# The mask of a causal attention added by TensorE: two full-array products per step against eight in 32x32 tiles

## The chip, the core and the metric

The kernel runs on one NeuronCore of a Trainium2 chip. The metric is the device time of one execution in microseconds (us). Engines are named as in the profile: PE is TensorE (its matmuls), PEld its weight loads, DVE is VectorE, ACT is ScalarE, POOL is GpSimd and SP is SyncE, whose queue issues most of the DMAs.

## What is computed

The reference is a two-layer block on x of shape 16 x 128 x 256 (16 batches of 128 tokens): a first attention with fp8-rounded projections, a gated feed-forward, a second attention, and a feed-forward over 8 experts. The change touches the second attention alone:

```
scores = einsum("bnghd,bmgd->bnghm", q, k) / sqrt(8)      # 32 heads of width 8, in 8 groups of 4
scores = where(attention_mask == 0, -inf, scores)          # per key of the batch
scores = where(tril(ones(128, 128)), scores, -inf)         # causal
attn = softmax(scores); out = einsum("bnghm,bmgd->bnghd", attn, v) @ w_o.T + b_o
```

## The kernel before

The second attention runs as a software pipeline over 64 steps n. Step n belongs to batch b = n // 4 and covers 8 of the 32 heads, as two groups of four. Four batches form a group g, for which `load`, `norm`, `turn` and `queries` (the front, spread over 16 steps by `front_step`) bring keys, values and queries into SBUF. The pipeline loop (L1291) calls for each n, in this order: `scores(n)`, `top(n)`, `probs(n - 1)`, `exp(n)`, `values(n - 2)`, `divide(n - 5)`, every fourth step `keys` of the next batch, then a piece of the next front, pieces of the routing for the experts (`route`), and every fourth step `output`. During the first steps, `down` finishes the feed-forward before.

The steps that matter here, by line:

- `load(g)` makes on DVE `pad` (L1062), which is 0 or -1e30 per key, and `comb` (L1063), the elementwise minimum of `pad` and the causal mask: 128 queries on the partitions, 4 batches x 128 keys in bf16, once per group.
- `scores(n)` fills a PSUM tile `ps_sc` of two banks, one for each group i of four heads, with 512 float32 per partition. First the mask goes in: for each i one bf16 matmul of the identity (`identb`, 128x128) with `comb` broadcast over four heads (L1141). Then the scores are added: for each i one float32 matmul with 32 contraction rows (L1148), which lie on the partitions 32 * (2p + i), where p = n % 2. A float32 matmul shows as two MATMUL records.
- `top(n)` takes on DVE the negated maximum per head (L1155). `exp(n)` is eight activations on ACT (L1164), one per head, which read `ps_sc` directly. `probs(n)` transposes the eight results on PE (L1175), and DVE (L1179) or, for a quarter of them, ACT (L1177) copies them out as `eT`.
- `values(n)`, for odd n, is four float32 matmuls with 32 output columns each (L1203): their results go to four different quarters of the PSUM partitions. ACT copies them out (L1209), and they go through DRAM and back to `divide` (L1236 on DVE, L1237 on POOL). `output` is L1243 on PE, `queries` L1103, `turn` L1092; the transposes of `route` are L159.
- `keys(b)` makes `kb` for a batch on POOL (L1118), the keys of a group multiplied with a head mask.

`ps_sc` has two buffers, `ps_tr` two, `ps_pv` one, `comb` two. The framework writes the order on each engine out ahead of time, from the priority in which the program issues instructions and from planned durations; the score matmuls get a raised priority (`tc.high_priority(offset=100)`). So each engine has a fixed order, and PE takes its matmuls in that order.

Of the kernel before, what the change touches and what calls it, by code (L numbers as in the profile page):

```python
# [9 lines left out]
F32 = mybir.dt.float32  # L10
F32R = mybir.dt.float32r
BF16 = mybir.dt.bfloat16
# [3 lines left out]
ALU = mybir.AluOpType  # L16
AX = mybir.AxisListType

P = 128
# [5 lines left out]
NEG = -1e30  # L25
# [10 lines left out]
def flamingo_kernel(  # L36
# [27 lines left out]
    nc = tc.nc  # L64
# [212 lines left out]
    with (  # L277
# [88 lines left out]
        class Unit:  # L366
# [15 lines left out]
            def load(self):  # L382
                b = self.b
                if self.cross:
                    cx = ap.tile([P, KD, P], F32, tag="ctx", name="ctx")
                    nc.sync.dma_start(out=cx, in_=kpn(ctxT)[:, :, b * P : (b + 1) * P])
                    xx = ap.tile([P, KD * P], F32R, tag="xx", name="xx")
                    nc.sync.dma_start(out=xx.bitcast(F32), in_=xqx[b])
                    self.kv_lhs = [cx[:, k, :] for k in range(KD)]
                    self.q_lhs = [xx[:, k * P : (k + 1) * P] for k in range(KD)]  # L390
# [160 lines left out]
            def scores(self, c):  # L551
                qT = self.qT.pop(c)
                pscore = ps_sc([P, 4, P])
                for j in range(4):
                    nc.tensor.matmul(  # L555
                        pscore[:, j, :], qT[:, j, :], self.kT[:, 2 * c + j // 2, :],
                        start=True, stop=True,
                    )
                self.sc[c] = pscore
# [244 lines left out]
    G = 4  # L804
    NT = G * P
# [75 lines left out]
    NQ = NH // NG  # L881
# [9 lines left out]
    for j in range(B):  # L891
# [9 lines left out]
        out=before, in_=ones, pattern=[[1, P]], compare_op=ALU.is_gt, fill=0.0,  # L901
        base=0, channel_multiplier=-1,
# [3 lines left out]
        rank, pattern=[[-1, NE]], base=NE, channel_multiplier=0,  # L906
# [4 lines left out]
        spare, pattern=[[P, B]], base=B * P, channel_multiplier=1,  # L911
# [10 lines left out]
    def route(b0, G):  # L922
# [73 lines left out]
    cq = f1.enter_context(tc.tile_pool(name="a1c", bufs=1, side="right", reuse_waits="tile"))  # L996
    gp = f1.enter_context(tc.tile_pool(name="a1f", bufs=2, side="right", reuse_waits="tile"))
# [7 lines left out]
    identb = cq.tile([P, P], BF16, name="identb")  # L1005
    nc.vector.tensor_copy(identb, ident)

    causal = cq.tile([P, P], F32, name="causal")
    nc.gpsimd.memset(causal, 0.0)
    nc.gpsimd.affine_select(  # L1010
        out=causal, in_=causal, pattern=[[-1, P]], compare_op=ALU.is_ge, fill=NEG,
        base=0, channel_multiplier=1,
    )

    hmask = cq.tile([P, NQ], F32, name="hmask")
    nc.vector.memset(hmask, 0.0)
    for q in range(P // 32):
# [3 lines left out]
            out=rows, in_=rows, pattern=[[-HD, NQ]], compare_op=ALU.is_ge, fill=0.0,  # L1021
            base=0, channel_multiplier=1,
        )
        nc.gpsimd.affine_select(
            out=rows, in_=rows, pattern=[[HD, NQ]], compare_op=ALU.is_ge, fill=0.0,
            base=HD - 1, channel_multiplier=-1,
# [16 lines left out]
    front = {}  # L1043

    def load(g):
        tok = slice(g * NT, (g + 1) * NT)
        kT = gp.tile([P, KD, NT], F32, tag="k", name="kT")
        for r in range(0, P, HD):
            q = r // 32
            nc.sync.dma_start(  # L1050
                out=kT[r : r + HD],
                in_=k1s.rearrange("(c q d) t -> q d c t", q=4, d=HD)[q][:, :, tok],
            )
        v = gp.tile([P, G, NG * HD], F32, tag="v", name="v")
        nc.sync.dma_start(out=v, in_=v1s[tok, :].rearrange("(b t) n -> t b n", t=P))
        mi = gp.tile([P, NT], I32, tag="mi", name="mi", bufs=1)
        nc.sync.dma_start(
            out=mi, in_=mask[g * NT : (g + 1) * NT].partition_broadcast(P)
        )
        comb = gp.tile([P, G, P], BF16, tag="comb", name="comb")  # L1060
        pad = gp.tile([P, NT], F32, tag="pad", name="pad", bufs=1)
        nc.vector.tensor_scalar(pad, mi, 0.0, NEG, ALU.is_equal, ALU.mult)  # L1062
        nc.vector.tensor_tensor(  # L1063
            comb, pad.rearrange("p (b t) -> p b t", b=G),
            causal[:, None, :].to_broadcast([P, G, P]), ALU.min,
        )
        front[g] = {"k": kT, "v": v, "comb": comb}

    def norm(g):
        rows = [x[b] for b in range(g * G, (g + 1) * G)]  # L1070
# [35 lines left out]
            )  # L1106
        nc.scalar.activation(f["q"][:, c, :], pm, AF.Copy, scale=SCALE1)

    kbs, vps, es, eTs, oTs, scs, mxs, ovs = {}, {}, {}, {}, {}, {}, {}, {}

    def keys(b):

        g, j = divmod(b, G)
        f = front[g]
        tok = slice(j * P, (j + 1) * P)
        kb = ap.tile([P, KD, NQ, P], F32, tag="kb", name="kb")
        for c in range(KD):
            nc.gpsimd.tensor_tensor(  # L1118
                kb[:, c], f["k"][:, c, None, tok].to_broadcast([P, NQ, P]),
                hmask[:, :, None].to_broadcast([P, NQ, P]), ALU.mult,  # L1120
            )
        v = f["v"][:, j, :].rearrange("p (g d) -> p g d", d=HD)
        if b < B - 1:
            nc.gpsimd.tensor_copy(vgs[b % 2][:, :, 0 : 2 * HD : 2], v)
        else:
            vp = vpad[:]
            nc.gpsimd.tensor_copy(
                bass.AP(vp.tensor, vp.offset, [vp.ap[0], [P, NG], [32 + HD, NQ], [1, HD]]),
                v[:, :, None, :].to_broadcast([P, NG, NQ, HD]),
            )  # L1130
        kbs[b], vps[b] = kb, vgs[b % 2]

    def scores(n):

        b, c, p = n // 4, n // 2 % 2, n % 2
        g, j = divmod(b, G)
        f = front[g]
        tok = slice(j * P, (j + 1) * P)
        s = psum.tile([P, 2, NQ, P], F32, tag="sc", name="ps_sc", bufs=2)
        for i in range(2):  # L1140
            nc.tensor.matmul(  # L1141
                s[:, i], identb, f["comb"][:, j, None, :].to_broadcast([P, NQ, P]),
                start=True, stop=False,
            )
        with tc.high_priority(offset=100):
            for i in range(2):
                rows = slice(32 * (2 * p + i), 32 * (2 * p + i) + 32)
                nc.tensor.matmul(  # L1148
                    s[:, i], f["q"][rows, c, tok], kbs[b][rows, c], start=False, stop=True
                )  # L1150
        scs[n] = s
# [105 lines left out]
    def front_step(g, i):  # L1257

        if i == 0:
            load(g)  # L1260
            norm(g)
        elif i == 3:
            turn(g)
        elif 5 <= i < 7:
            queries(g, i - 5)

    hds = {}
    for g in range(B // G):
# [3 lines left out]
        for b in range(g * G, (g + 1) * G):  # L1272
# [11 lines left out]
            name="psum1", bufs=1, space=bass.MemoryType.PSUM, reuse_waits="tile"  # L1284
# [6 lines left out]
    for n in range(-2, N1 + 2):  # L1291
        if 0 <= n < N1:
            scores(n)
            top(n)
# [14 lines left out]
        if m % 4 == 0 and 0 <= m < N1:  # L1309
            keys(m // 4)  # L1310
        g, i = divmod(n + 12, 16)
# [14 lines left out]
    for stages in routes:  # L1326
        for _ in stages:
# [6 lines left out]
            name="psum2", bufs=2, space=bass.MemoryType.PSUM, reuse_waits="tile"  # L1334
# [6 lines left out]
    for e in range(NE):  # L1341
# [6 lines left out]
            out=xe, in_=disp[e * CAP : (e + 1) * CAP, :].rearrange("(c p) d -> p c d", p=P)  # L1348
# [5 lines left out]
        for f in range(NFC):  # L1354
            ph = ps_mm([P, CAP])
            for k in range(KD):
                nc.tensor.matmul(
                    ph, w1t[:, k, f * P : (f + 1) * P], xT[:, k, :],
                    start=(k == 0), stop=(k == KD - 1),
# [3 lines left out]
        for c in range(NCC):  # L1363
            po = ps_sc([P, DM])
            for f in range(NFC):
                nc.tensor.matmul(
                    po, hT[:, f, c * P : (c + 1) * P], w2t[:, f, :],
                    start=(f == 0), stop=(f == NFC - 1),
# [6 lines left out]
                out=out_rows,  # L1375
# [3 lines left out]
                in_=oe[:, c, :],  # L1379
# [77 lines left out]
```

## Time and profile before

| | us |
|---|---|
| median of 3 runs | 1472.05 |
| the runs, from and to | 1471.78 to 1472.88 |
| the profiled execution's own time | 1470.57 |
| its span, first to last instruction | 1468.9 |
| TensorE clock granted, mean | 0.979 |
| second attention, L1141 from its first to its last start | 1044.4 to 1308.8 |

The profile is of one execution. "Busy" counts instructions of an engine; matmuls are pipelined and their ends are modelled, so a PE record is longer than the time until the next matmul may begin. What a matmul costs in a stream is therefore read from the starts: the start of the next instruction minus its own. The busy shares of the whole span are PE 93%, DVE 67%, ACT 57%, POOL 46%.

### The profile page before, as it was taken

The numbers are of one execution on the slowest core, as the hardware profiler recorded it, in microseconds if no ns is written. First come the engines' busy times: TensorE is split into PE (matmuls) and PEld (weight loads), VectorE is DVE, ScalarE is ACT, GpSimd is POOL, SyncE is SP. The second block draws the span as 40 slices with busy tenths as digits, with TensorE's granted clock in tenths as the row PEclk, the third lists the DMA queues.
The fourth block names the chain that finished last, engine by engine and source line by source line (L and its number), as shares of the span: only waits on it lengthen the run. The fifth ranks groups of instructions, "written<-read, shape, count | busy, mean of one in ns | idle before, by whom it ended". The sixth has DMA issues, their size and how long they took to land. (4 is left out here: it accounts for less than half of the span.)

```text
span 1468.9 us, 22241 instructions
## 1 busy us (share of the span) xinstructions
PE 1371.6 (93%) x7112; PEld 972.6 (66%) x7112; DVE 988.7 (67%) x2604; ACT 840.2 (57%) x2505; POOL 681.6 (46%) x641
## 2 busy tenths in 40 slices
PE   6799999999989899999999997999999999996998
PEld 5577787878766677777777765455544544455887
DVE  6788888887887677677776775453467877882110
ACT  5666666666656566666666663163467666751211
POOL 1576877777777456556556564121031422211111
PEclk9899999999999999999999999999999999996999
DMA  5201001000031100000000000700042222122562
GB/s 176 87 20 39 26 24 35 26 21 26 24 112 53 36 22 15 12 19 16 14 20 12 15 4 27 216 8 15 4 150 56 66 61 66 44 63 93 190 196 66
DMA packets 77844, 79.88 MB, mean 54 GB/s; under 512 B 15131, under 2 KB 63963, under 8 KB 77728
## 3 DMA queue, kind: packets, MB, share of 16 engines
q1 hardware_dynamic: 64224, 54.76, 13.0%
q10 hardware_dynamic: 11456, 17.63, 3.7%
q0 software_dynamic: 2048, 6.07, 1.1%
q8 instruction: 57, 0.93, 0.3%
q14 instruction: 59, 0.48, 0.1%
HBM read 56.88 MB, written 21.79 MB: 54 GB/s over the span
## 5 line engine op out<-in xcount | busy, mean ns | idle before, releaser
L525 POOL TENSOR_TENSOR raw<-raw,q_r 128x512 f32<-128x512 f32 x192 | 220.2, 1168 | 8.6 <-DVE q_r L340 7.6
L583 POOL TENSOR_TENSOR e<-e,sums 128x512 f32<-128x512 f32 x128 | 135.8, 1061 | 182.9 <-ACT raw L485 73.9
L571 ACT ACTIVATE e<-ps_sc,mx 128x128 f32<-128x128 f32 x512 | 181.1, 368 | 65.1 <-DVE mx L563 63.9
L494 DVE BATCH_NORM_STATS2 q_st<-raw 128x6 f32<-128x128 f32 x768 | 172.3, 278 | 59.2 <-ACT raw L485 58.9
L645 PE MATMUL ps_acc<-wp,cat 128*128 128x512 f32 x512 | 160.0, 435 | 18.4 <-POOL cat L260 17.5
L596 ACT COPY eT<-ps_tr 128x512 f32<-128x512 f32 x128 | 75.3, 588 | 171.4 <-PE ps_tr L594 171.4
L260 POOL TENSOR_TENSOR cat<-e_t,e_e 128x1024 fp32r<-128x1024 bf16 x64 | 136.6, 2135 | 53.2 <-DVE e_t L254 51.4
L1164 ACT ACTIVATE e<-ps_sc,mx 128x128 f32<-128x128 f32 x512 | 139.1, 391 | 27.2 <-DVE mx L1155 26.8
L555 PEld LDWEIGHTS ps_sc<-kT,qT 128*128 128x128 f32 x1024 | 132.2, 193 | 28.9 <-ACT qT L546 20.6
L555 PE MATMUL ps_sc<-kT,qT 128*128 128x128 f32 x1024 | 140.6, 280 | 6.6 <-ACT qT L546 6.5
L537 PE MATMUL ps_tr<-ident,raw 128*128 128x128 f32 x768 | 113.4, 277 | 24.1 <-ACT kT L546 15.3
L645 PEld LDWEIGHTS ps_acc<-wp,cat 128*128 128x128 f32 x512 | 93.7, 191 | 61.9 <-POOL cat L260 28.7
L604 PE MATMUL ps_pv<-eT,vt 128*128 128x256 f32 x512 | 133.1, 381 | 1.0 <-DVE cat_y L615 1.0
L537 PEld LDWEIGHTS ps_tr<-ident,raw 128*128 128x128 f32 x768 | 92.4, 142 | 56.3 <-issue 26.7
L485 ACT COPY raw<-ps_mm 128x512 f32<-128x512 f32 x192 | 113.7, 593 | 24.8 <-PE ps_mm L473 21.6
L604 PEld LDWEIGHTS ps_pv<-eT,vt 128*128 128x128 f32 x512 | 96.7, 191 | 31.2 <-issue 11.1
L615 DVE TENSOR_TENSOR cat_y<-ps_pv,r_sm 128x512 bf16<-128x512 f32 x128 | 87.1, 680 | 44.8 <-PE ps_pv L604 44.8
L546 ACT ACTIVATE qT<-ps_tr,hv 128x512 f32<-128x512 f32 x128 | 101.5, 793 | 20.4 <-PE ps_tr L537 16.7
L571 ACT ACTIVATION_READ_ACCUMULATOR e<-ps_sc,mx 128x1 f32 x512 | 105.3, 206 | 0.0
L563 DVE TENSOR_REDUCE mx<-ps_sc 128x4 f32<-128x512 f32 x128 | 87.1, 680 | 25.8 <-PE ps_sc L555 25.8
L1175 PEld LDWEIGHTS ps_tr<-ident,e 128*128 128x128 f32 x512 | 59.4, 141 | 62.5 <-ACT e L1164 25.1
L1155 DVE TENSOR_REDUCE mx<-ps_sc 128x8 f32<-128x1024 f32 x64 | 77.5, 1211 | 27.0 <-PE ps_sc L1148 18.5
(249 smaller groups left out, 2701.4 us busy)
## 6 DMA issues: line engine op xcount, KB each, us to landing
w1t<-in_w ACTq DMA_DIRECT2D x8, 1024.0 KB
w2t<-in_w ACTq DMA_DIRECT2D x8, 1024.0 KB
disp<-empty SPq DMA_DIRECT2D x16, 257.0 KB
xe<-disp SPq DMA_DIRECT2D x8, 514.0 KB
stage<-in_wprojT SPq DMA_DIRECT2D x16, 256.0 KB
ctx<-in_ctxT SPq DMA_DIRECT2D x32, 128.0 KB
ods<-og SPq DMA_DIRECT2D x120, 32.0 KB
ov<-ods SPq DMA_DIRECT2D x30, 128.0 KB
```

Of the source, the lines that this page charges most:

```text
L260: ins = nc.gpsimd.tensor_tensor(dsts[i], t[:, part], e[:, part], ALU.subtract)
L485: nc.scalar.copy(raw.rearrange("p h d -> p (h d)"), pm)
L494: nc.vector.bn_stats(self.st[:, 4 * blk + j, :], self.raws[blk][:, j, :])
L525: ins = nc.gpsimd.tensor_tensor(src, src, self.r[:, 4 * blk : 4 * blk + 4, None].to_broadcast([P, 4, P]), ALU.mult,)
L537: nc.tensor.transpose(pt[:, j, :], src[:, j, :], ident)
L546: nc.scalar.activation(dst, pt, AF.Identity, scale=hv[:, col : col + 1], bias=hv[:, col + 1 : col + 2])
L555: nc.tensor.matmul(pscore[:, j, :], qT[:, j, :], self.kT[:, 2 * c + j // 2, :], start=True, stop=True,)
L571: nc.scalar.activation(e[:, j, :], pscore[:, j, :], AF.Exp, bias=self.mx[:, j : j + 1], accum_out=sums[:, j : j + 1],)
L583: divs[n] = nc.gpsimd.tensor_tensor(e, e, sums[:, :, None].to_broadcast([P, 4, P]), ALU.mult)
L604: nc.tensor.matmul(pv[:, 2 * g : 2 * g + 2, :], self.vt[:, gg * P : (gg + 1) * P], eT[:, 2 * g : 2 * g + 2, :], start=True, stop=True,)
L645: nc.tensor.matmul(self.acc, self.cat[c // 2][:, h % 8, :], wpr[self.cross, c][:, j, :, :], start=(h == 0), stop=(h == 15),)
L1164: nc.scalar.activation(e[:, i, :], s[:, i // NQ, i % NQ, :], AF.Exp, bias=mx[:, i : i + 1])
```

## The change

The mask's products are made in 32x32 tiles of the PE array instead of the whole array. For each step and each i, the one 128x128 product becomes four, one for each quarter k of the 128 queries: 32 contraction rows on the partitions 32 * (2p + i), the same partitions that the score matmul of this i uses, and 32 output columns, so that quarter k of the queries lands on the PSUM partitions 32k to 32k + 31. All eight of a step name different 32x32 tiles of the array: two groups of rows by four groups of columns.

For that the mask is laid out differently: every quarter of the SBUF partitions holds the whole mask of 128 queries, with quarter k of the queries at column block k. `causal` becomes a bf16 tile of 128 x (4 x 128), made once by four POOL instructions instead of one. `comb` has the same size as before (128 x 512 bf16) but now holds one batch in place of four. It is made in `keys(b)`, once per batch, 16 times instead of 4, from `pad` and `causal`, which are both bf16 now (both were float32). `pad` gets a second buffer.

```
-    causal = cq.tile([P, P], F32, name="causal")
+    causal = cq.tile([P, 4, P], BF16, name="causal")
     nc.gpsimd.memset(causal, 0.0)
-    nc.gpsimd.affine_select(
-        out=causal, in_=causal, pattern=[[-1, P]], compare_op=ALU.is_ge, fill=NEG,
-        base=0, channel_multiplier=1,
-    )
+    for r in range(0, P, 32):
+        nc.gpsimd.affine_select(
+            out=causal[r : r + 32], in_=causal[r : r + 32], pattern=[[32, 4], [-1, P]],
+            compare_op=ALU.is_ge, fill=NEG, base=0, channel_multiplier=1,
+        )
...
-        comb = gp.tile([P, G, P], BF16, tag="comb", name="comb")
-        pad = gp.tile([P, NT], F32, tag="pad", name="pad", bufs=1)
+        pad = gp.tile([P, NT], BF16, tag="pad", name="pad")
         nc.vector.tensor_scalar(pad, mi, 0.0, NEG, ALU.is_equal, ALU.mult)
-        nc.vector.tensor_tensor(
-            comb, pad.rearrange("p (b t) -> p b t", b=G),
-            causal[:, None, :].to_broadcast([P, G, P]), ALU.min,
-        )
-        front[g] = {"k": kT, "v": v, "comb": comb}
+        front[g] = {"k": kT, "v": v, "pad": pad}
...
     def keys(b):
...
+        combs[b] = gp.tile([P, 4, P], BF16, tag="comb", name="comb")
+        nc.vector.tensor_tensor(
+            combs[b], f["pad"][:, None, tok].to_broadcast([P, 4, P]), causal, ALU.min
+        )
...
         s = psum.tile([P, 2, NQ, P], F32, tag="sc", name="ps_sc", bufs=2)
-        for i in range(2):
-            nc.tensor.matmul(
-                s[:, i], identb, f["comb"][:, j, None, :].to_broadcast([P, NQ, P]),
-                start=True, stop=False,
-            )
+        for k in range(4):
+            for i in range(2):
+                r = 32 * (2 * p + i)
+                nc.tensor.matmul(
+                    s[32 * k : 32 * k + 32, i], identb[r : r + 32, r : r + 32],
+                    combs[b][r : r + 32, k, None, :].to_broadcast([32, NQ, P]),
+                    start=True, stop=False,
+                )
```

## The prediction

> **What bounds the kernel now.** I read the page first (PE busy 93% of the span), then the sums for the second attention, 1044 to 1311 us, the only stretch that the change touches:
>
> ```profile
> core 0: us, PE busy (x) PEld busy (x) DVE busy (x) ACT busy (x) POOL busy (x), PEclk, DMA share, GB/s
> 1044.00:1311.00 267.00, 264.24 (x1363) 126.22 (x1361) 202.57 (x377) 177.05 (x590) 67.66 (x91) 0.99 0.25 69
> ```
>
> PE is almost never seen idle, DVE is busy for 76%, ACT for 66%. Since matmul records overlap, I took the order in time of PE over a few steps:
>
> ```profile
> 1186.73 0.59 PE L1141 MATMUL ps_sc<-comb,identb 128*128 128x512 bf16 x2
> 1187.25 1.13 PE L1148 MATMUL ps_sc<-kb,qT 32*128 32x512 f32 x4
> 1188.31 1.66 PE L1175 MATMUL ps_tr<-ident,e 128*128 128x128 f32 x8
> 1189.90 1.06 PE L1203 MATMUL ps_pv<-eT,vg 128*32 128x512 f32 x8
> 1190.89 1.13 PE L1243 MATMUL ps_mm<-ao,oT 128*128 128x256 f32 x4
> ...
> 1198.54 0.60 PE L1141 MATMUL ps_sc<-comb,identb 128*128 128x512 bf16 x2
> 1199.08 1.13 PE L1148 MATMUL ps_sc<-kb,qT 32*128 32x512 f32 x4
> 1200.13 1.10 PE L1175 MATMUL ps_tr<-ident,e 128*128 128x128 f32 x8
> 1201.07 0.59 PE L1141 MATMUL ps_sc<-comb,identb 128*128 128x512 bf16 x2
> ```
>
> Columns: start, length, engine and line. Starts give the cost: mask to score 0.52, score to transposes 1.06, eight transposes 0.94 when nothing holds them (1200.13 to 1201.07) but 1.59 at 1188.31. There they are paced by ACT, whose eight exponentials come 0.26 apart. Of the 61 transposed steps that run unbroken in the timeline, 41 take about 0.82 from first to last start, PE's own pace, and 20 take 1.33 to 1.81; the 20 hold PE up by 13.9 us in all. So PE sets the end most of the time, and the chain maximum, exponential, transpose for a third of the steps. Who holds that chain up is in the waits of the maximum and of the exponential:
>
> ```profile
> L1164 ACT ACTIVATE e<-ps_sc,mx 128x128 f32<-128x128 f32 x502 | 136.4, 391 | 27.2 <-DVE mx L1155 26.8 <-DVE slot_s L980 0.2
> L1155 DVE TENSOR_REDUCE mx<-ps_sc 128x8 f32<-128x1024 f32 x64 | 77.5, 1211 | 27.0 <-PE ps_sc L1148 18.5 <-ACT qT L1107 3.6 <-ACT e L1164 2.4
> ```
>
> Only 21 of the 64 maxima wait for PE's scores (18.5 us); at the others DVE was still at something else. A score that is ready sooner helps the exponential at about a third of the steps.
>
> **PE, what is removed.** Two products of 0.216 us each (the two starts 1191.86 and 1192.08), and from the second to the first score 0.309. The second product streams 0.216 of that; the other 0.093 is PE emptying before the array changes from 128 rows to 32. The same 0.09 shows wherever the shape changes: eight transposes take 0.93 to the next full-array product, 1.02 to a 32-column product (1153.13 to 1154.15). Mask to score is 0.216 + 0.309 = 0.525.
>
> **PE, what is added.** No 32x32 product is in this trace. The nearest rows are L1203, four products on four groups of columns, and L1148, two on two groups of rows:
>
> ```profile
> 1189.89:1189.93 0.04, 0.03 (x4) 0.03 (x5) 1.00 0.09 26
> ```
>
> The first bracket counts matmuls: four of L1203 begin within this 0.04 us, 0.007 apart; the whole of `values` takes 0.99 (1189.90 to 1190.89) where its eight records of 0.43 would need 3.4 in a row. Column groups overlap, and L1148 shows the same for row groups: two pairs in 1.06. So I take all eight as overlapping: seven gaps of 0.007, one stream of 0.216, one emptying of 0.093, together 0.36 in place of 0.525: 0.167 less. But the array now also changes shape in front of the mask. Of the 64 masks, 16 follow `values`, where the change of shape is paid already; 48 follow transposes, output or queries at full size, where it is new: 0.093 more. PE's work falls by 16 x 0.167 + 48 x 0.074 = 6.2 us. The bounds: 0.27 to the score if 32x32 to 32x128 needs no emptying (then 64 x 0.255 - 48 x 0.093 = 11.9 us less), and eight streams in a row, 8 x 0.216 + 0.093 = 1.82, 83 us more. I take the overlap, since each kind of split is seen overlapping by itself. The 12 further weight loads a step (the 32-column ones last 0.109) begin with their products, as those of L1203 do, and cost nothing beyond the 0.007; without that cover they would cost at most their length.
>
> A page of the Trainium skill speaks against this: "TensorE: Matmul & The Clock Gate", section "Wait — 56ns, not 53.3ns?", says that matmul starts never come closer than about 25 ns. The four starts within 0.04 us contradict it here (its Part 3 gives about 4 ns for products of different tiles). By the page eight tiles would take 7 x 0.025 + 0.216 + 0.093 = 0.48, which by this estimate loses 0.05 at 48 masks and gains 0.04 at 16, so PE would have 1.7 us more.
>
> **How much of 6.2 us arrives.** Not all: PE time saved before an ACT-paced burst (20 steps, 1.5 us at 0.074) turns into waiting, which leaves 4.7 at most. Where DVE is late, the exponential and what follows stay where they were: at the low end only the 21 steps whose maximum waits for PE gain, 21 x 0.097 (the mean of 6.2 over 64) = 2.0. I take 3.0, nearer the low end, since the steps that follow `values`, with the largest saving, are also those that lead into the ACT-paced bursts.
>
> **DVE.** `comb` is made 16 times in place of 4. The row of before, with float32 inputs:
>
> ```profile
> L1063 DVE TENSOR_TENSOR comb<-pad,causal 128x512 bf16<-128x512 f32 x4 | 2.7, 667 | 0.0
> ```
>
> With bf16 inputs the nearest row is a bf16 TENSOR_TENSOR of twice the elements, 689 ns (L254, 128x1024 bf16, on `in_y`); float32 at 128x256 is 425 (L868). 256 float32 elements more cost 0.24, so 0.18 is fixed; (0.69 - 0.18) / 2 + 0.18 = 0.43 for 512 in bf16. DVE gets 16 x 0.43 - 2.7 = 4.2 us more, 8.0 at the float32 rate. `comb` stands in DVE's queue behind the copies of step 4b - 3 and ahead of a maximum; what is queued behind it is the maximum, and behind that the exponential. DVE is idle for 27.0 us in front of the maxima, 1.7 per batch, against 0.26 more work per batch. So most of it is covered; at the third of the steps where the chain sets the end it is not: 4.2 / 3 = 1.4, less what the four removed ones no longer hold, so 1.2 (0.3 to 2.5). Its buffer comes free with the scores of batch b - 2, long done. DVE loses the wait that `comb` had, for PE's use of the group before last, with nothing visible in front of it (0.0 idle in the row).
>
> **At nothing:** `pad` in bf16 (four of 0.7 us, same count); the four selects on POOL, between 0.8 (L1020, 0.196 each) and 1.5 us (L1010, 0.36 each), at 919 to 925 us, 45 us before the mask is first read and with POOL at one tenth busy. No DMA is added or moved.
>
> **Sum** against the profiled execution's 1470.57: -3.0 + 1.2 = -1.8, 1468.8. The median of the runs stands 1.5 higher, so 1470.3.
>
> **Rivals.**
> 1. More arrives, 1467.3: 32x32 to 32x128 keeps the row split and empties nothing. Then 11.9 us go from PE; half of it, as above, is 5.9, less 1.2 of DVE. For it: both shapes use 32 rows. Against it: every change of shape in the trace, of rows or columns alone, costs 0.09.
> 2. Slower, 1478.4: the eight tiles go in two rounds, since both kinds of split at once were never seen. Place: between the first mask start and the first score, 0.05 + 2 x 0.216 + 0.093 = 0.57 in place of 0.525; with the 48 new changes of shape PE has 64 x 0.046 + 4.5 = 7.4 us more, of which I let 5.1 through (what is lost on PE is hidden less often than what is gained), plus 1.2. It decides as soon as mask to score exceeds 0.46, where PE's gain is gone. Against it: two splits that each overlap alone. A full row of eight, 1.82, would be some 1550.
> 3. DVE becomes the bound, 1476: `comb` at the float32 rate directly ahead of the maxima, 8.0 us with nothing hidden, less some 4 of PE. It decides if the order leaves DVE no idle time at that place; 1.7 us a batch speaks against it.
> 4. The order on PE is laid out anew, and foreign work falls between the eight small products as it does now between the two in 4 of 64 steps. Each such break costs two changes of shape, 0.19: under 2 us unless it becomes the rule.
>
> **How the numbers follow.** The sum 0.42 (its own range 1467.7 to 1472.6, from the ends 2.0 to 4.7 and 0.3 to 2.5); rival 1 0.24; rival 2 0.17; rival 3 0.12; rival 4 and others 0.05. A measurement of this kernel can tell about 0.2%, 2.9 us, from no change: faster means under 1469.1, slower over 1475.0. Faster: 0.14 of the sum, rival 1, 0.02 of the rest: 0.40. Same: 0.28 of the sum, 0.03 of rival 3, 0.02: 0.33. Slower: rival 2, 0.09 of rival 3, 0.01: 0.27. From 1466.0 to 1478.0 I leave out the better half of rival 1 and the worse half of rival 2.
>
> **What the profile after would show.** Right: eight mask starts within 0.06 us, first score 0.36 after the first of them, transposes to mask 0.20 where it was 0.11; 16 `comb` of 0.43; more than 20 ACT-paced bursts. Wrong: mask starts in two clusters, mask to score near 0.27 or 0.57, `comb` at 0.67, or a maximum that waits on DVE's `comb` in most batches.

## The result, and the profile after

The changed kernel takes 1490.12 us in the median of five runs (1483.58 to 1493.8) against 1472.35 for the kernel before beside it: a ratio of 1.0104 with a 95% interval of 1.0085 to 1.0123. Slower by 17.8 us, where 1.8 faster was forecast; the range given ended at 1478.0. The profiled execution took 1491.41 us, span 1489.7 (before: 1468.9). The runs of one kernel differ in their granted clock, and in time with it (before, 25 runs on one chip: from 1471.3 us at 0.979 to 1477.3 at 0.973), so a profile, which is of one run, can lie several us from the median.

First the mechanism, in PE's order in time of the changed kernel (start, length, engine and line; the mask is L1144, scores L1152, transposes L1179, values L1207, output L1247):

```profile
1199.35 1.06 PE L1207 MATMUL ps_pv<-eT,vg 128*32 128x512 f32 x8
1200.34 1.13 PE L1247 MATMUL ps_mm<-ao,oT 128*128 128x256 f32 x4
1201.40 0.41 PE L1144 MATMUL ps_sc<-comb,identb 32*32 32x512 bf16 x8
1201.74 1.13 PE L1152 MATMUL ps_sc<-kb,qT 32*128 32x512 f32 x4
1202.80 1.09 PE L1179 MATMUL ps_tr<-ident,e 128*128 128x128 f32 x8
1203.82 0.41 PE L1144 MATMUL ps_sc<-comb,identb 32*32 32x512 bf16 x8
```

The eight products are one record of 0.41 us. The count by stretches shows all eight starts inside 0.04 us:

```profile
1201.39:1201.43 0.04, 0.03 (x8) 0.03 (x8) 1.00 0.00 0
```

Mask to score is 0.34 (1201.40 to 1201.74) where it was 0.525. All of that is as forecast. What was not is in the sums for the stage, from the first mask product to the last (PE, PEld, DVE, ACT and POOL busy, then the granted clock, DMA share, GB/s); the first line is of after, the second of the same stretch of before:

```profile
1050.30:1330.30 280.00, 272.00 (x1737) 129.08 (x1736) 207.35 (x383) 177.87 (x587) 68.33 (x91) 0.94 0.24 67
```
```profile
1044.40:1308.80 264.40, 261.64 (x1352) 125.36 (x1351) 200.40 (x373) 175.01 (x583) 67.66 (x91) 0.99 0.25 70
```

From start to start of the mask products the stage has 280.0 us for 264.5: it is 15.5 us longer, its clock 0.94 instead of 0.99, and it begins 5.9 us later (1050.3 for 1044.4). The page's slices show where the clock went (before first, then after; a digit is a 40th of the span, 8 is 80 to 90% of full speed):

```profile
PEclk9899999999999999999999999999999999996999
```
```profile
PEclk9899999999999999999999998999999898897999
```

Slices 32, 34 and 35 of after lie in the stage. The groups of the exponential, the maximum and the mask on DVE, in after (busy, mean ns | idle in front and what ended it):

```profile
L1168 ACT ACTIVATE e<-ps_sc,mx 128x128 f32<-128x128 f32 x512 | 139.4, 390 | 46.0 <-DVE mx L1159 45.5 <-issue 0.3
L1159 DVE TENSOR_REDUCE mx<-ps_sc 128x8 f32<-128x1024 f32 x64 | 77.5, 1211 | 30.3 <-PE ps_sc L1152 24.8 <-ACT e L1168 4.4 <-ACT og L1213 0.7
L1114 DVE TENSOR_TENSOR comb<-pad,causal 128x512 bf16<-128x512 bf16 x16 | 9.9, 618 | 1.5 <-PE ps_sc L1144 1.5
```

ACT now waits 45.5 us for maxima where it waited 26.8. The worst place is near 1258 us. DVE first, then PE:

```profile
1253.89 0.69 DVE L1183 COPY eT<-ps_tr 128x512 f32<-128x512 f32 x1 [0.15 <-issue]
1258.21 0.17 DVE L977 COPY row<-number 128x2 int32<-128x2 int32 x1 [3.63 <-DMA disp<-row,slot_s]
1258.29 0.42 DVE L1249 TENSOR_TENSOR t<-ps_mm,bo 128x256 f32<-128x256 f32 x1
1258.74 0.48 DVE L1254 SCALAR_TENSOR_TENSOR row<-t,tg,x 128x256 f32<-128x256 f32 x1
1259.26 0.43 DVE L142 BATCH_NORM_STATS2 ln_st<-row 128x6 f32<-128x256 f32 x1
1259.60 0.94 DVE L1240 RECIPROCAL rsum<-ov 128x128 f32<-128x128 f32 x1
1260.46 0.12 DVE L143 BATCH_NORM_AGGREGATE ln_mv<-ln_st 128x2 f32<-128x6 f32 x1
1260.50 1.19 DVE L1159 TENSOR_REDUCE mx<-ps_sc 128x8 f32<-128x1024 f32 x1
```
```profile
1258.60 1.13 PE L1152 MATMUL ps_sc<-kb,qT 32*128 32x512 f32 x4
1262.14 2.28 PE L1179 MATMUL ps_tr<-ident,e 128*128 128x128 f32 x8 [2.41 <-ACT e L1168]
```

A tiny copy of the token numbers into the router's row (L977) stands at the head of DVE's queue and waits 3.63 us for the scatters that read the row buffer's last contents. The maximum is queued behind it, and behind that the exponential and PE, which waits 2.41. In this stage of after the copy waits twice, 3.53 us at 1186.80 and the 3.63 here. Before has such waits too, but shorter ones, 2.73 and 1.99; the first of them:

```profile
1177.77 0.17 DVE L977 COPY row<-number 128x4 int32<-128x4 int32 x1 [2.73 <-DMA ods<-og]
```

The next lines are the windows around the wait in after:

```profile
1254.86:1258.27 3.41, 3.41 (x27) 1.87 (x28) 0.06 (x1) 1.15 (x4) 0.63 (x2) 1.00 0.49 160
1258.27:1261.68 3.41, 1.46 (x13) 0.40 (x12) 3.34 (x8) 0.58 (x1) 1.05 (x2) 1.00 0.24 62
1261.68:1265.10 3.42, 2.96 (x12) 1.66 (x16) 3.42 (x6) 2.75 (x11) 1.39 (x2) 0.51 0.21 54
1265.10:1275.34 10.24, 10.24 (x52) 4.58 (x48) 5.18 (x7) 5.39 (x20) 0.45 (x1) 0.50 0.12 26
1275.34:1278.75 3.41, 3.41 (x12) 1.18 (x4) 0.59 (x1) 2.08 (x7) 0.24 (x1) 0.50 0.02 5
```

PE is busy for 1.46 of 3.41 us, and from the end of that window the clock (third column from the end) is one half for 17.1 us: a wait of 2.4 us is followed by a loss several times as long.

**An account of the stage.** From the starts and the clock records I split each profile's stage in three: *idle*, time between two PE starts beyond the first one's stream and 0.095 us for a change of shape; *half*, the time at half clock, of which half is lost; and *rest* = stage - idle - half/2, which is PE's own work.

| kernel | first mask | stage | idle | half | rest |
|---|---|---|---|---|---|
| before | 1044.4 | 264.5 | 38.8 | 3.4 | 224.0 |
| after | 1050.3 | 280.0 | 47.5 | 34.1 | 215.5 |
| after, again | 1050.7 | 279.8 | 47.6 | 34.1 | 215.1 |

PE's work falls by 8.5 us; its waiting grows by 8.7; and (34.1 - 3.4)/2 = 15.4 go to the clock. Together 15.6 of the 15.5. The split charges half of the half clock as lost even where PE was waiting in it (2.3 us of after's idle time, 0.3 of before's). Counted start by start, with the clock that each start had, PE's work falls by 7.3, waiting grows by 8.6 and the clock takes 14.1. Apart from the mask's products, and those without use that some later runs add to the router, the stage holds the same matmuls in all 16 profiles, so these differences are not work that moved in or out of it.

### The profile page after: what moved, and what is told of

The parts are those of the page before. It is cut to its first block, busy times and chain, and to the rows that moved or that the text cites. A ratio compares the mean times of both kernels' runs of the same rounds, so it can differ in the third digit from the quotient of the medians.

```text
span 1489.7 us, 23028 instructions
## 1 busy us (share of the span) xinstructions
PE 1385.2 (93%) x7496; PEld 979.7 (66%) x7496; DVE 994.2 (67%) x2612; ACT 843.3 (57%) x2509; POOL 684.0 (46%) x644
## 5 line engine op out<-in xcount | busy, mean ns | idle before, releaser
L1168 ACT ACTIVATE e<-ps_sc,mx 128x128 f32<-128x128 f32 x512 | 139.4, 390 | 46.0 <-DVE mx L1159 45.5
L260 POOL TENSOR_TENSOR cat<-e_t,e_e 128x1024 fp32r<-128x1024 bf16 x64 | 136.6, 2135 | 54.4 <-DVE e_t L254 51.7
L555 PEld LDWEIGHTS ps_sc<-kT,qT 128*128 128x128 f32 x1024 | 133.3, 195 | 28.8 <-ACT qT L546 20.5
L615 DVE TENSOR_TENSOR cat_y<-ps_pv,r_sm 128x512 bf16<-128x512 f32 x128 | 87.1, 680 | 45.5 <-PE ps_pv L604 45.5
L1179 PEld LDWEIGHTS ps_tr<-ident,e 128*128 128x128 f32 x512 | 63.5, 147 | 71.0 <-ACT e L1168 34.2
L1179 PE MATMUL ps_tr<-ident,e 128*128 128x128 f32 x512 | 93.5, 308 | 6.7 <-ACT e L1168 5.7
```

The source lines that it names most:

```text
L260: ins = nc.gpsimd.tensor_tensor(dsts[i], t[:, part], e[:, part], ALU.subtract)
L555: nc.tensor.matmul(pscore[:, j, :], qT[:, j, :], self.kT[:, 2 * c + j // 2, :], start=True, stop=True,)
L1168: nc.scalar.activation(e[:, i, :], s[:, i // NQ, i % NQ, :], AF.Exp, bias=mx[:, i : i + 1])
L1179: nc.tensor.transpose(pt[:, h, :], e[:, NQ * i + h, :], ident)
```

## Experiments

Theories: **C**, the clock (small products and waits let the array stream too little); **D**, DVE's mask per batch; **S**, the eight instructions and changes of shape in themselves. Later ones are named where they arise. Every ratio is to the kernel before on the same chip; the table at the end of this section gives the stages.

**The two parts apart.** First the mask per batch in bf16 on DVE, added by two full-array products (`causal` is here made by one select of 128x512 instead of four):

```
-        for k in range(4):
-            for i in range(2): ... 32x32 products ...
+        for i in range(2):
+            nc.tensor.matmul(s[:, i], identb,
+                combs[b][:, 0, None, :].to_broadcast([P, NQ, P]), start=True, stop=False)
```

> The DVE part alone: the combined mask is made per batch, 128x512 in bf16, 16 times, as in the changed kernel, but the products are the two full-array ones of before. Theory C (clock): the small products leave PE's array streaming for a smaller share of the time, so more stretches fall below what the clock gate asks for, and the 18 us are time at half clock; then this kernel is near before, 1472 to 1477 us, mean granted clock 0.975 or more. Theory D (DVE): the mask per batch and the order of instructions that comes with it delay the maxima, PE stands still, and the clock only follows; then 1483 to 1492 us and 0.970 or less.

Measured: 1476.23 us, 1.0008 (0.9992 to 1.0024). DVE's part by itself costs 1.2 us by the middle value, 3.5 by the upper end.

Then the small products with `causal` as their operand, so that DVE makes nothing per batch (the padding part of the mask is left out):

```
-        combs[b] = gp.tile([P, 4, P], BF16, tag="comb", name="comb")
-        nc.vector.tensor_tensor(combs[b], ...)
+        combs[b] = causal
```

> The PE part alone: the small products of the changed kernel, with the causal mask as their operand, so no mask is made on DVE in the second attention at all (the padding mask is left out). Theory C: still slow, 1480 to 1492 us, granted clock 0.973 or less, since the small products are there. Theory D: DVE has less to do than before the change, so 1468 to 1473 us and 0.978 or more.

Measured: 1486.54 us, 1.0082 (1.0058 to 1.0105). Most of the loss comes with the small products, though they take PE's own work down to 215.2 us in the stage.

**Are the products dear in themselves?** The eight issued twice:

```
                     combs[b][r : r + 32, k, None, :].to_broadcast([32, NQ, P]),
-                    start=True, stop=False,
+                    start=True, stop=True,
...
+        (the same two loops once more, with stop=False)
```

> The changed kernel with each group of eight small products issued twice in a row (the second overwrites the first): PE streams some 0.22 us more per step, as long as the two full-array products did. By itself that is up to 64 x 0.22 = 14 us of PE work, of which a third to three quarters would show. Theory C: the streaming share is that of before, the clock comes back to 0.976 or more, 1474 to 1482 us, less than the changed kernel although it does more. Theory D: nothing is cured, 1490 to 1500 us.

Measured: 1524.19 us, 1.0337 (1.0311 to 1.0364). PE's rest rises by 6.7 us to 222.2 (64 more streams of 0.21 would be 13.6; 12.5 us of the idle time lie in half clock, and counted start by start PE's work rises by 11.4), but the time rises by 34 against the changed kernel: idle 54.4, half clock 68.3. My expectation from C, that more streaming would hold the clock, is wrong as I put it. A third of the added time is the products themselves, the rest is again waiting and clock; why these grow when PE's steps become longer is not shown.

The kernel before with its products split by columns alone, eight of 128x32 in a step, with the same changes of shape:

```
+            for k in range(4):
                 nc.tensor.matmul(
-                    s[:, i], identb, f["comb"][:, j, None, :]...
+                    s[32 * k : 32 * k + 32, i], identb[:, 32 * k : 32 * k + 32], f["comb"][:, j, None, :]...
```

> Before, with each full-array product split by columns alone: four products of 128 rows x 32 columns, eight per step as in the changed kernel, and the same 48 further changes of the array's shape, but in two rounds of 0.216 us, so that PE streams as long as before; mask layout and DVE work are those of before. Theory C: 1472 to 1478 us (48 x 0.093 = 4.5 us more on PE, partly hidden), clock 0.976 or more. A third theory, S, that eight small instructions and the changes of shape are the cost in themselves, gives 1483 to 1492 us.

Measured: 1481.76 us, 1.0031 (1.0012 to 1.0051). Its rest is 227.7, 3.7 above before, where 48 new changes of shape at 0.093 make 4.5; its idle time, 38.6, is that of before. So S is real and small, and is contained in the prediction's sum. This kernel has the waits of the copy at L977 as after has them, 3.53 and 3.70 us, the second of them here:

```profile
1251.39 0.17 DVE L977 COPY row<-number 128x2 int32<-128x2 int32 x1 [3.70 <-DMA disp<-row,slot_s]
```

But each is followed by only 3.4 us of half clock, where after has 3.4 and 17.1. The small products without DVE's mask have waits of 3.79 and 3.88 there, and 3.4 and 17.1 us behind them. So the long waits alone do not make the loss of after; they make it together with the small products.

The changed kernel once more, as a control beside the next two:

> The changed kernel once more, on the chip and in the call of the next two, for a second profile: 1484 to 1494 us, and some 30 us of half clock in the second attention. If the half-clock stretches lie elsewhere than in the first profile, they are chance; if they begin at the same three waits for a maximum (steps where the copy of the token numbers for the router stands ahead of it on DVE), these waits are their cause.

Measured: 1491.05 us, 1.0111 (1.0066 to 1.0156); the same stage to 0.2 us, with the same 34.1 us of half clock at the same four places: 20.5 us behind the two waits at L977 (from 1190.3 and 1262.0) and 13.7 behind the router's products (from 1159.6 and 1231.3).

**The wait at L977.** The copy is tied behind the router's last weight, which comes later in DVE's queue, in both kernels:

```
-        nc.vector.tensor_scalar(row[:, :, 2 * DM], s1, tg[:, 3:4], None, ALU.mult)
-        nc.vector.tensor_copy(row[:, :, 2 * DM + 1].bitcast(I32), number[:, gsl])
+        weight = nc.vector.tensor_scalar(row[:, :, 2 * DM], s1, tg[:, 3:4], None, ALU.mult)
+        stay_after(nc.vector.tensor_copy(row[:, :, 2 * DM + 1].bitcast(I32), number[:, gsl]), weight)
```

> The changed kernel with one instruction of the router, the copy of the token numbers (L977), tied behind the router's weight, so that DVE no longer waits for it, and for the DMAs that free its row buffer, ahead of a maximum. Theory G: the 18 us are PE waits of 1.4 to 2.5 us at these places and the half clock that follows where the small products keep PE's streaming share low; without the waits 1470 to 1478 us, half clock in the second attention under 14 us. Theory H: the small products lose by themselves, wait or no wait: 1482 us or more and over 25 us of half clock.

> The kernel before with the same copy tied behind the router's weight. Its profile has one such wait (2.1 us, then 3.4 us at half clock), so both theories expect little: 0 to 4 us less than before, 1468 to 1476 us.

Measured: the changed kernel falls to 1477.02 us, 1.0021 (0.9995 to 1.0047); the kernel before to 1467.06, 0.9943 (0.9923 to 0.9963), which beats both kernels. In after, 14 us by the medians hang on the waits at this copy and the half clock behind them. (The profiled run of the tied kernel, 1483.42, is one of its slower ones; between the profiles the stage is 8.1 shorter. The groups of small products are broken at the same ten places as before the tie.) In the kernel before, the wait at 1177.77 has 3.4 us of half clock behind it. But the quotient of the two edited kernels is 1.0021 / 0.9943 = 1.0078 (1.004 to 1.011 with both intervals): some 11 us remain that are not this wait.

**What the rest is.** Three theories. **V**: DVE's mask per batch. **O**: foreign work between the small products (in after other work stands at 10 places, in 7 steps, between a step's eight products, in before at 4 between its two). **C** again, now at the router's 16 products of 8 columns, where the clock of the edited changed kernel drops (at 1159.2 and 1227.5). Its order there, and the clock behind it:

```profile
1155.52 0.39 PE L1146 MATMUL ps_sc<-comb,identb 32*32 32x512 bf16 x1
1155.83 1.14 PE L1181 MATMUL ps_tr<-ident,e 128*128 128x128 f32 x8
1156.81 1.85 PE L935 MATMUL ps_mm<-wgt,rT 128*128 128x8 f32 x16
1158.59 0.40 PE L1146 MATMUL ps_sc<-comb,identb 32*32 32x512 bf16 x7
```
```profile
1155.80:1159.20 3.40, 3.40 (x34) 3.06 (x35) 1.33 (x6) 3.15 (x11) 3.02 (x3) 1.00 0.34 87
1159.20:1166.10 6.90, 6.90 (x22) 2.63 (x21) 5.60 (x21) 2.83 (x10) 2.52 (x4) 0.51 0.01 1
```

PE counts as busy throughout, and still the clock falls: the router's products last 1.85 us and stream 16 x 8 columns.

O: the last seven products are placed directly behind the first.

```
+                with tc.high_priority(offset=100 if first else 0):
                     ins = nc.tensor.matmul(... 32x32 product ...)
+                if first: stay_after(ins, first)
+                else: first = ins
```

> The changed kernel with the row copy tied, and the eight small products of a step kept together: each of the last seven is placed directly behind the first, so that no transposes, values or router work stand between them (ten groups were broken before). Without this edit the kernel took 1477.0 us, 20.5 us of it at half clock within the second attention; the kernel before with the copy tied takes 1467.1. Theory O (the order on PE: foreign work between the small products makes PE wait inside a group and thins out the windows in front of each drop of the clock): 1462 to 1470 us, half clock under 7 us in the stage, and no wait of PE at a mask group. Theory C (the small products carry too little for the clock wherever they stand): 1474 to 1480, half clock over 12 us. Theory V (the mask made per batch on DVE makes the maxima late): 1474 to 1480 with waits of PE for exponentials of 4 us or more in the stage and half clock unchanged.

C: full-array products without use among the router's, in both edited kernels.

```
+        wide = ps("mm", [P, 512], 1)
+        lg = wide[:, 0 : G * NE].rearrange("p (g e) -> p g e", e=NE)
         for j in range(G):
+            nc.tensor.matmul(wide[:, P:], identb, identb[:, None, :].to_broadcast([P, 3, P]), start=True, stop=True)
```

> The changed kernel with the row copy tied, and with useless full-array products in the router: one bf16 product of 128x384 columns in front of the router's products of each batch, into unused columns of the same PSUM tile, 0.16 us each, 0.64 us at each group of four batches, 2.6 us of PE in all. The drops of the clock at 1159 and 1227 us follow directly on the windows of the router's 16 products of 8 columns, where the array streamed 0.41 to 0.44 of the time. Theory C (a window that streams too little costs half clock afterwards): with 0.6 in those windows these two drops go, half clock in the stage falls from 20.5 us to under 10, and the time is 1472 to 1476, faster than without the useless work. Theories O and V: the work adds what it takes, 1478 to 1481, with the same waits.

> The kernel before with the row copy tied, and the same useless products in the router. It has no half clock in the stage without them (1467.1 us). All theories: 2 to 4 us more, 1468 to 1471, since there is no half clock to be saved; a gain would show that the useless work does something else than to hold the clock.

V: the first experiment with the copy tied.

> The row copy tied, the mask made per batch in bf16 on DVE as in the change, but added by two full-array products as before. Theory V (DVE's work per batch is what is left of the loss): 1473 to 1478. Theories O and C (the small products, by order or by clock): 1466 to 1470, with half clock under 5 us in the stage.

Measured: groups kept whole 1478.57, 1.0032 (1.0013 to 1.0051); with the filling 1476.51, 1.0021 (1.0004 to 1.0039); before with the filling 1467.44, 0.995 (0.9935 to 0.9966); DVE's part 1471.69, 0.9979 (0.9967 to 0.9991).

O is wrong: no group is broken any more and no time is won. C is right in the clock and not in the time: both router drops went (half clock 20.5 to 3.4 us in the stage) with PE 2.6 us more to do, and the median did not move against the kernel without the filling. V holds in part: 0.9979 / 0.9943 = 1.0036, some 5 us of the 11 (2 to 9 with both intervals).

**The start of the stage.** The first mask begins later in every kernel with the four selects beside DVE's layer norm: 1048.7 to 1051.4 in eight profiles, against 1044.4 to 1047.9 in the six others. The program on PE up to there is the same. POOL and PE of after, then PE of before:

```profile
924.46 2.74 POOL L1012 TENSOR_SCALAR_AFFINE_SELECT causal<-causal 32x512 bf16<-32x512 bf16 x4
```
```profile
924.41 2.32 PE L159 MATMUL ps_tr<-ident,ln_y 128*128 128x128 f32 x8 [1.73 <-DVE ln_y L148]
928.64 1.76 PE L159 MATMUL ps_tr<-ident,ln_y 128*128 128x128 f32 x7 [1.91 <-DVE hT L160]
```
```profile
919.49 1.48 PE L159 MATMUL ps_tr<-ident,ln_y 128*128 128x128 f32 x8 [1.46 <-DVE ln_y L148]
```

and DVE's layer norm beside them, before and then after:

```profile
919.35 2.52 DVE L148 TENSOR_SCALAR ln_y<-x,ln_mv,ln_r 128x256 f32<-128x256 f32 x7
```
```profile
924.28 3.71 DVE L148 TENSOR_SCALAR ln_y<-x,ln_mv,ln_r 128x256 f32<-128x256 f32 x7
```

Of the 5.9 us, 4.9 are there when the first of these transposes starts (924.41 for 919.49), ahead of the first select; so the selects do not make them. The kernel before with the copy tied, whose program is that of before up to there, starts these transposes as late as 922.9. After has also had 10.8 us of half clock since 880 us by then, before 3.4. The two stretches that differ, near 886 and 907 us, stand in all eight profiles with the four selects, but also in two of the eight others; what brings them is not shown.

What the selects do is the rest. Seven steps take 3.71 us instead of 2.52, and PE, which transposes their results, loses 1.2 (from the first of the 15 transposes to the last 5.57 us, for 4.36). In the records one by one, a step takes 0.40 us alone, and 0.72 to 0.76 when a select starts just ahead of it, ending 0.15 after the select each time. The Trainium skill ("SBUF — State Buffer", section "SBUF: two separate sides") says that a GpSimd instruction and a DVE instruction in a 2-port mode (or one with two SBUF inputs, if the GpSimd instruction reads SBUF) exclude each other from a shared pair of SBUF ports, for the whole of the instruction that starts first. These records fit it; that the layer-norm step is in such a mode is not shown.

Three runs for what was still open: the small products without DVE's mask and with the copy tied (the padding part left out); the changed kernel with copy tied, groups whole and the selects behind the other constants; and that with the filling as well.

```
-        nc.gpsimd.affine_select(out=causal[r : r + 32], ...)
+        select = nc.gpsimd.affine_select(out=causal[r : r + 32], ...)
+        stay_after(select, dsb_tg)
```

> The row copy tied, the mask added in eight small products, but with causal as their operand, so that DVE makes no mask per batch (the padding part of the mask is left out). Theory V (the mask made on DVE is what makes PE wait more): idle time of PE in the stage back to 36 to 39 us, as in the kernel before with the copy tied (36.0), and 1463 to 1468 us. Theory W (the work that the small products take off PE turns into waiting for the exponentials, whoever makes the mask): idle 42 to 46 us, and 1470 to 1476, with half clock of 5 to 20 us in the stage.

> The changed kernel with the row copy tied, its small products kept together, and the four selects that make causal on POOL placed behind the other constants, so that they no longer run beside DVE's seven layer-norm steps at 924 us. If they slow those steps (0.53 us each in the changed kernel, 0.36 in the one before), the eight plus seven transposes there go from 5.57 to 4.36 us, the first mask product starts 1 to 2 us earlier (1050.4 without this edit), and the time is 1474 to 1478 (1478.6 without). If the selects have nothing to do with it, the transposes stay at 5.57.

> The changed kernel with all four edits: row copy tied, small products kept together, selects placed later, and the useless full-array products in the router. Theory W with the clock repaired: half clock in the stage under 7 us, PE's idle time in the stage still 44 to 47 us, 1471 to 1476: still slower than the kernel before with the row copy tied alone (1467.1). If the small products bring what was predicted once nothing else is in the way, 1462 to 1467.

Measured: 1469.26, 0.9982 (0.996 to 1.0003); 1480.1, 1.004 (1.0018 to 1.0062); 1471.69, 0.9987 (0.9974 to 1.0001). With the selects moved the 15 transposes take 4.33 and 4.32 us, so the 1.2 us are settled by the trace; the first mask starts at 1045.2 and 1047.8, but there too most of the gain is ahead of the transposes (920.5 and 923.0). The median did not fall by moving the selects (1480.1 for 1478.57 with groups whole alone, on another chip). The kernel with all four repairs is some 17 us faster than after by the ratios, and not slower than before by anything that can be told; beside the kernel before with one of them it still loses, 0.9987 / 0.9943 = 1.0044, some 6 us (3 to 10 with both intervals). The spans of the two profiles differ by 2.7 of that. In their stages half clock is 3.4 us and none; idle is 42.8 against 36.0 (just under the 44 to 47 that W gave), which takes nearly all of the 7.2 us by which PE's rest is shorter. Without DVE's mask idle is 41.2, between what V (36 to 39) and W (42 to 46, the saved work turns into waiting) expected; 1469.26 lies just below W's range. Its quotient, 0.9982 / 0.9943 = 1.0039, stands beside the 1.0036 of DVE's part: with the copy tied each part costs some 5 us by itself, and together they make the 1.0078 of both.

| kernel | time | profiled run | first mask | stage | idle | half | rest |
|---|---|---|---|---|---|---|---|
| DVE part alone | 1476.23 | 1479.64 | 1047.9 | 270.9 | 42.0 | 10.2 | 223.8 |
| small products alone | 1486.54 | 1486.25 | 1048.7 | 276.4 | 45.9 | 30.7 | 215.2 |
| small products twice | 1524.19 | 1522.18 | 1050.9 | 310.8 | 54.4 | 68.3 | 222.2 |
| columns only | 1481.76 | 1481.55 | 1047.7 | 273.2 | 38.6 | 13.7 | 227.7 |
| before, copy tied | 1467.06 | 1468.21 | 1047.5 | 260.2 | 36.0 | 0.0 | 224.2 |
| same, router filled | 1467.44 | 1466.73 | 1047.2 | 259.0 | 36.2 | 0.0 | 222.8 |
| DVE part, copy tied | 1471.69 | 1471.64 | 1045.2 | 265.3 | 37.9 | 6.8 | 224.0 |
| after, copy tied | 1477.02 | 1483.42 | 1050.1 | 271.9 | 45.5 | 20.5 | 216.2 |
| and groups whole | 1478.57 | 1480.87 | 1050.4 | 269.1 | 45.9 | 10.2 | 218.1 |
| after, copy tied, router filled | 1476.51 | 1481.3 | 1051.2 | 268.7 | 46.8 | 3.4 | 220.2 |
| small products, copy tied | 1469.26 | 1478.49 | 1051.4 | 266.0 | 41.2 | 17.1 | 216.3 |
| groups whole, selects moved | 1480.1 | 1471.8 | 1045.2 | 265.1 | 43.8 | 6.8 | 217.9 |
| all four | 1471.69 | 1470.94 | 1047.8 | 261.6 | 42.8 | 3.4 | 217.0 |

The time is a median over 4 to 12 runs, the other columns are of the one profiled run. For "small products, copy tied" that run is one of four at 1478.5 to 1480.1 us, with a granted clock of 0.971, while the other eight took 1467.5 to 1470.4 at 0.975 to 0.980.

## Why the prediction was wrong, step by step

**What was right.** The picture of PE: eight starts within 0.023 us (0.06 forecast), first score 0.338 after the first (0.36), transposes to mask 0.202 (0.20), one emptying at each change of shape. Rival 2, two rounds, is excluded by the starts, rival 1 by the gap of 0.315 from the last mask start to the score. PE's own work fell by 8.5 us by the table, 7.3 counted start by start, where 6.2 was forecast. (The products added per step are six, and so are the weight loads, not 12 as written; nothing hung on it.) The side, slower, had 0.27, but most of it for a mechanism that did not occur.

**The step that failed first: "How much of 6.2 us arrives".** It took 3.0, between 2.0 and 4.7. Nothing arrived: idle rose by 8.7 us. By place, PE's waits inside the transposes' bursts rose by 2.2 us (17.9 to 20.1), those in front of a first transpose by 4.1 (3.0 to 7.1), and those of mask groups broken by layer-norm transposes by 1.6. The part that the wait at L977 does not touch is seen with the copy tied: the small products alone take 7.9 us off PE's rest and add 5.2 of idle time (41.2 for 36.0), and lose what is left, and more, to 17.1 us of half clock; DVE's part alone adds 1.9. The prediction let savings vanish only before the 20 bursts that ACT already paced. But the chain of maximum, exponential and transpose did not become shorter with PE's work, and the waits for it grew: ACT's wait for maxima went from 26.8 to 45.5 us. With half clock nearly gone (all four repairs) the trade is the same, 7.2 less work and 6.8 more waiting beside the kernel before with the copy tied.

**The term that was missing: the clock.** The sum held PE's clock constant. The page of before showed a full clock in nearly the whole stage, which I read as a property of the stage; it was the result of how much the array streamed, and the change makes it stream less. At 14 to 15 us this is the largest term. I summed for each window of 3.413 us, between 400 and 1325 us of the 16 profiles, the share of time in which the array streamed (0.21 us for 512 columns of bf16, 0.43 of float32, 0.107 for a transpose). Of 4129 windows at full clock, 101 streamed under 0.40, and 100 of them were followed by half clock; between 0.40 and 0.46 it was 19 of 56; above, 7 of some 3970, and none above 0.55. The router's windows of before lie at 0.45, just above the edge, as could have been worked out from its trace. The Trainium skill has this window of 3413 ns, running freely ("TensorE: Matmul & The Clock Gate", Part 1, "What's actually happening"), but as its abstract rule it asks for no idle gap of PE over about 3.4 us ("HAM oscillation — how this bites in real kernels"). The longest wait of PE in this stage is 2.5 us, so by that rule nothing drops; the windows above show that a half-filled one is enough.

**A wait in a queue that the sum did not walk through.** DVE was costed by its added time, 4.2 us, not by who stands behind whom. With the order laid out anew, L977 came to the head of DVE's queue before its row buffer was free, 7.2 us in two waits where before has 4.7 in two, with the maxima behind it. 14 us hang on it, most of it through the clock: 20.5 of the 34.1 us of half clock stand behind these two waits.

**"At nothing".** The four selects were priced by length, 0.8 to 1.5 us, and took 2.6; what counted was the place, beside DVE's layer norm. Of the 5.9 us by which the stage begins late, 1.2 are this. The group means of the first masks differ by 3.8 (1050.5 with the selects there, 1046.7 in the six others), but 2.5 of that is there when the first transpose starts, ahead of the selects; the cause of this part stays open.

**A mis-sized term: DVE's mask.** 0.43 us each was right for 11 of the 16 (0.36 to 0.43). The other five start just behind a POOL instruction, in four cases a product for the keys, and take 0.68 to 1.27; each of them ends 0.28 us after that instruction. So the mean is 0.618 and DVE has 9.9 - 2.7 = 7.2 us more, not 4.2. The trace of before could have warned: its row L254, taken at 0.689 us on `in_y`, has 1.034 on `cat_y`, for the same shape. The part that shows, 1.2, is what the first experiment measured; where the wait at L977 is gone, it is some 5.

**What stays open.** By idle time the two parts add up: with the copy tied either alone adds 5.2 and 1.9 us to the 36.0 of before, and all four repairs leave 42.8. Which waits inside the chain take the 5.2 is not taken apart further, nor why "small products twice" waits and loses clock as it does, nor what shifts the start of the stage ahead of the selects. Rival 4 priced a break at 0.19 us; there were ten, and mending them won nothing that could be measured.

## To carry to other kernels

When PE paces a stage only two thirds of the time, look for what waits next before counting a saving of PE: here 8.5 us less work became 8.7 us more waiting. Sum the array's streaming over 3.4-us windows; where some lie near 0.45, shorter products and longer waits can fall under the edge: here that cost some 14 us, and a saving on PE became a loss. A small instruction that waits for a buffer belongs behind the work of others in its engine's queue: that one tie made the kernel before 0.6% faster (0.9943), more than the change was meant to gain.

## What the runs showed of the hardware

- The clock falls after windows that stream under about 0.42 of the time, without any idle gap of a window's length, and its return needs much more: of 207 windows at half clock, none of the 53 under 0.75 was followed by full clock, 36 of 54 at 0.85 to 0.90, and 81 of 87 above. A single wait of 2.4 us was followed by 17.1 us at half clock.
- Useless full-array products, some 2.6 us of them (an estimate: 16 of 0.16, from 0.216 for 512 columns), take away half clock (20.5 to 3.4 us in the stage of one profile); the time did not improve, so this is not a gain that was shown.
- Eight products on eight different 32x32 tiles start 3 ns apart and stream together.
- DVE's bf16 mask takes 0.36 to 0.43 us, and up to 1.27 when it starts just behind a POOL instruction, after whose end it then needs 0.28; DVE's layer-norm step takes 0.40 alone and 0.72 to 0.76 just behind a select, after whose end it needs 0.15.
- Every change between products of 128x128, 32x128, 128x32 and 32x32 costs PE some 0.095 us: the last transpose to the mask is 0.109 before and 0.202 after.
